# Layer 1's attention with normalised weights that carry the shared part, on column groups of TensorE

## The chip, the cores and the metric

The kernel runs on one core of a Trainium2 chip. Its engines are TensorE (PE; its weight loads are listed apart as PEld), VectorE (DVE), ScalarE (ACT), GpSimd (POOL) and SyncE (SP), which here issues most DMAs. [...] The metric is the device time of one execution in microseconds. Before the change it is 4359.8 us, the median of 3 runs (4357.15 to 4369.78).

## The reference

Two graph layers on 64 graphs of 256 nodes and 512 features, all in fp32, 8 heads of 64 features each.

```python
# layer 0: x = layernorm(x + relu(attention)), W of 512 x 64 per head
feats = einsum('bnf,hfu->bhnu', X, W)
dense = leaky_relu(e_self[..., :, None] + e_neigh[..., None, :], 0.2)
att   = softmax(dense + NEG_BIG * (1 - A), axis=-1)
out   = relu(einsum('bhij,bhju->bhiu', att, feats) + b)

# layer 1: x = layernorm(x + out @ W_out + b_out)
dots = einsum('bhid,bhjd->bhij', q, k) * scale      # q, k, v from x @ W_qkv
attn = softmax(where(m2, dots, -big), axis=-1) * 0.33
attn = attn + 0.33 * adj + 0.33 * exp(-dist)        # adj = dist = A, masked by m2
out  = einsum('bhij,bhjd->bhid', attn, v)
```

In layer 1 the last two terms of `attn` are the same for all heads of a graph: the shared part, `CT` in the kernel.

## The kernel before

A graph's 256 nodes are two tiles of 128 (T = 2), its 512 features four (C = 4). Per graph there are four lists of steps. `proj0` turns x (pt_x, L154), makes the logits (pe, L246), turns the adjacency (pa, L215) and makes from it `AT` and `CT`, makes the rows of the logits (pr, L259) and sends them through DRAM to all partitions (gs, then gb; L273 and L274), computes from them the columns ccol and wcol (nd, L279; L284, L285), and makes the features (pf, L290), which POOL scales by wcol into `V0` (L298). `attend0` makes the weights pT on DVE (L324) and multiplies them with V0 in `weighted` (av_h0, L167): a tile of weights is the stationary operand, 128 by 128, and the values of a head, 64 columns and one for the sum, the moving one. `proj1` turns the result (pt_h, L154) and makes q and k (pq, L372) and v (pv, L386). `attend1` makes the scores transposed (pz, L415), two heads on two halves of the array's rows, the exponentials on ACT (L425), and the values by the same `weighted` (av_h1, L167), with a column of ones in V1 for the sums. DVE then divides by the sums (L436 to L439). `rest` multiplies CT with V1 for all heads (pcv, L450) and DVE adds it (L457). The result o is turned (pt_o, L154, copied by ACT at L157), projected (po, L472), added and normalised.

`together` (L502) interleaves two lists by their counts of steps. In turn b, `attend0(b)` goes with `proj1(b-1)`, then `attend1(b-1)` with `proj0(b+1)`. A tile framework then sets the final order on each engine and the semaphores. On SP stand, in that order, the loads of x, adjacency and mask, gs and gb, and the store of y.

Of the kernel before, what the change touches and what calls it, by code (L numbers as in the profile page):

```python
# [8 lines left out]
FT = mybir.dt.float32  # L9
U8 = mybir.dt.uint8  # L10
AF = mybir.ActivationFunctionType
ALU = mybir.AluOpType
# [4 lines left out]
def kernel(  # L17
# [21 lines left out]

    nc = tc.nc  # L40
# [25 lines left out]
    def ps_tile(shape, tag, name):  # L66
        return psum.tile(shape, FT, tag=tag, name=name)
# [44 lines left out]
    nc.vector.memset(neg, -NEG)  # L112
    mhalf = consts.tile([P, T], FT, name="mhalf")
# [4 lines left out]
    for s, a in enumerate((a_self, a_neigh)):  # L118
        a_bc = work.tile([P, H, U], FT, tag="oT", name=f"a_bc_{s}", bufs=1)
        nc.sync.dma_start(  # L120
            a_bc.rearrange("p h u -> p (h u)"),
            a.rearrange("h u -> (h u)").partition_broadcast(P),
        )
        for c in range(C):
            prod = work.tile([P, H, U], FT, tag="o", name=f"prod_{c}_{s}")
            nc.vector.tensor_mul(prod, w0_sb[:, c], a_bc)
            nc.vector.tensor_reduce(wa[:, c, s], prod, AX.X, ALU.add)
# [16 lines left out]
    mla = consts.tile([P, T, NB], FT, name="mla")  # L144
    nc.vector.tensor_scalar_mul(mla, pm, LA)
# [51 lines left out]
    V0, GB, CCOL, AT, CT = {}, {}, {}, {}, {}  # L197

    def proj0(b):
# [3 lines left out]
        GB[b] = work.tile([P, H, N + 1], FT, tag="gb", name=f"gb_{b}")  # L203
        AT[b] = work.tile([P, T, N], FT, tag="at", name=f"at_{b}")
        CT[b] = work.tile([P, T, N], FT, tag="ct", name=f"ct_{b}", bufs=3)
# [5 lines left out]
        def adjacency():  # L211
# [12 lines left out]
            mrow = small.tile([P, N], FT, tag="mrow", name=f"mrow_{b}", bufs=2)  # L224
            nc.gpsimd.tensor_copy(mrow, MROW[b])
            for j in range(T):
# [8 lines left out]

            nc.gpsimd.tensor_scalar(
                mrow, mrow, -LA / N, LA / N, op0=ALU.mult, op1=ALU.add
            )
            for j in range(T):
                nc.gpsimd.tensor_add(CT[b][:, j, :], CT[b][:, j, :], mrow)  # L240
# [46 lines left out]
        def features(t):  # L287
# [9 lines left out]
            nc.scalar.copy(feat[:, t].rearrange("p h u -> p (h u)"), pf)  # L297
            nc.gpsimd.tensor_mul(  # L298
# [7 lines left out]
            *(lambda t=t: tr(t) for t in range(T)),  # L306
            logits,
            adjacency,
            rows,
            *(lambda t=t: features(t) for t in range(T)),  # L310
# [5 lines left out]
    def attend0(b):  # L316
        o = work.tile([P, T, F], FT, tag="o", name=f"o0_{b}")
# [36 lines left out]
        for g in range(2):  # L354
            steps += [lambda h=h: weights(h) for h in range(g * HG, (g + 1) * HG)]
            steps += [lambda g=g, t=t: values(g, t) for t in range(T)]
        return steps + [end]
# [4 lines left out]
    def proj1(b):  # L362
        hT = work.tile([P, C, N], FT, tag="xT", name=f"hT_{b}")
        QK[b] = work.tile([P, HG, 2, N], FT, tag="qk", name=f"qk_{b}")
        V1[b] = work.tile([P, T, H, UA], FT, tag="v1", name=f"v1_{b}")
# [17 lines left out]
        def values(t):  # L383
            pv = ps_tile([P, F], "mm", f"pv_{b}_{t}")
            for c in range(C):
                nc.tensor.matmul(  # L386
                    pv,
                    hT[:, c, t * P : (t + 1) * P],
                    wqkv_sb[:, c, 2].rearrange("p h u -> p (h u)"),
                    start=(c == 0),  # L390
                    stop=(c == C - 1),
                )
            nc.scalar.copy(
                V1[b][:, t, :, :U], pv.rearrange("p (h u) -> p h u", u=U)
            )
            nc.gpsimd.memset(V1[b][:, t, :, U], 1.0)

        return [
            *(lambda t=t: tr(t) for t in range(T)),
            *(lambda g=g: qk(g) for g in range(HG)),  # L400
            *(lambda t=t: values(t) for t in range(T)),
        ]


    def attend1(b):
        o = work.tile([P, T, F], FT, tag="o", name=f"o1_{b}")
        probs = {}

        def scores(g):

            pz = [ps_tile([P, T, N], "sc", f"pz_{b}_{2 * g + r}") for r in range(2)]
            for j in range(T):
                for r in range(2):
                    rows = slice(r * U, (r + 1) * U)
                    nc.tensor.matmul(  # L415
                        pz[r][:, j, :],
# [5 lines left out]
            for r in range(2):  # L422
                p = work.tile([P, T, N], FT, tag="p", name=f"p_{b}_{2 * g + r}", bufs=6)
                for j in range(T):
                    nc.scalar.activation(  # L425
                        p[:, j, :],
                        pz[r][:, j, :],
                        AF.Exp,
                        bias=hide[:, j, b : b + 1],
                    )  # L430
                probs[2 * g + r] = p

        def values(g, t):
            av = weighted(g, t, probs, V1[b], b, "h1")
            rec = small.tile([P, HG], FT, tag="rec", name=f"rec1_{b}_{g}_{t}")
            nc.vector.tensor_scalar_max(rec, av[:, :, U], TINY)  # L436
            nc.vector.reciprocal(rec, rec)
            nc.vector.tensor_scalar_mul(rec, rec, mla[:, t, b : b + 1])
            nc.vector.tensor_mul(  # L439
                o[:, t, g * HG * U : (g + 1) * HG * U].rearrange(  # L440
                    "p (h u) -> p h u", u=U
                ),
                av[:, :, :U],
                rec.unsqueeze(2).to_broadcast([P, HG, U]),
            )

        def rest(t):
            pc = ps_tile([P, H, U], "mm", f"pcv_{b}_{t}")
            for j in range(T):
                nc.tensor.matmul(  # L450
                    pc,
                    CT[b][:, j, t * P : (t + 1) * P],
                    V1[b][:, j, :, :U],
                    start=(j == 0),
                    stop=(j == T - 1),
                )
            nc.vector.tensor_add(  # L457
                o[:, t, :], pc.rearrange("p h u -> p (h u)"), o[:, t, :]
            )

        oT = work.tile([P, C, N], FT, tag="oT", name=f"oT_{b}", bufs=1)
        y = io.tile([P, T, F], FT, tag="y", name=f"y_{b}", bufs=2)
        tr = transposed(o, oT, b, "o")
# [17 lines left out]
        def end():  # L481
            layernorm(y, X1[b], b, "l1")
            nc.sync.dma_start(out[b].rearrange("(t p) f -> p t f", p=P), y)

        return [
            residual,
            lambda: scores(0),
            lambda: scores(1),
            lambda: scores(2),
            lambda: values(0, 0),  # L490
            lambda: values(0, 1),
            lambda: scores(3),
            lambda: values(1, 0),
            lambda: values(1, 1),
            *(lambda t=t: rest(t) for t in range(T)),
            *(lambda t=t: tr(t) for t in range(T)),
            *(lambda t=t: project(t) for t in range(T)),
            end,
# [3 lines left out]
    def together(one, two):  # L502
        n = len(one) + len(two)
        i = j = 0
        for _ in range(n):
            if j >= len(two) or (i < len(one) and i * len(two) <= j * len(one)):
                one[i]()
                i += 1
            else:
                two[j]()  # L510
                j += 1
# [3 lines left out]
    together(proj0(0), [])  # L515
    for b in range(NB + 1):
        if b + 2 < NB:
            load(b + 2)
        together(
            attend0(b) if b < NB else [],  # L520
            proj1(b - 1) if b >= 1 else [],
        )
        together(
            attend1(b - 1) if b >= 1 else [],
# [50 lines left out]
```

## Time and profile before

| | |
|---|---|
| median of 3 runs | 4359.8 us |
| the profiled execution | 4358.81 us |
| its span, first to last instruction | 4357.0 us |
| mean granted TensorE clock | 0.949 |
| VectorE busy | 37% |
| ScalarE busy | 23% |
| GpSimd busy | 19% |
| DMA moved, mean | 163.54 MB, 38 GB/s |

The costliest groups of TensorE by line, in us of busy time and mean length of one:

| line | what | instructions | busy | mean ns |
|---|---|---|---|---|
| L372 | q and k (pq) | 4096 | 927.4 | 382 |
| L167 | values of layer 1 (av_h1) | 4096 | 625.6 | 314 |
| L167 | values of layer 0 (av_h0) | 4096 | 487.9 | 272 |
| L386, L290, L472 | pv, pf, po | 1024 each | 463.6, 462.4, 460.2 | 595, 594, 592 |
| L415 | scores (pz) | 2048 | 427.8 | 456 |
| L450 | shared part (pcv) | 512 | 270.4 | 655 |

Matmuls overlap, so the length of one is not the time that it costs. That time is the distance from its start to the next one's, which the timeline gives.

### The profile page before, as it was taken

The numbers are of one execution on the slowest core, as the hardware profiler recorded it, in microseconds if no ns is written. First come the engines' busy times: TensorE is split into PE (matmuls) and PEld (weight loads), VectorE is DVE, ScalarE is ACT, GpSimd is POOL, SyncE is SP. The second block draws the span as 40 slices with busy tenths as digits, with TensorE's granted clock in tenths as the row PEclk, the third lists the DMA queues.
The fourth block names the chain that finished last, engine by engine and source line by source line (L and its number), as shares of the span: only waits on it lengthen the run. The fifth ranks groups of instructions, "written<-read, shape, count | busy, mean of one in ns | idle before, by whom it ended". The sixth has DMA issues, their size and how long they took to land.

```text
span 4357.0 us, 52007 instructions
## 1 busy us (share of the span) xinstructions
PE 4305.3 (99%) x20994; PEld 3126.9 (72%) x20994; DVE 1606.5 (37%) x4251; ACT 1021.7 (23%) x2241; POOL 819.7 (19%) x1286
## 2 busy tenths in 40 slices
PE   6999999999999999999999999999999999999999
PEld 4777777777777777777777777777777777777776
DVE  4333334334343333333433333334333333333342
ACT  1222222222222222222222222222222222222222
POOL 2112112111121221211212112122121121211211
PEclk9999999999999999999999999999999999999999
DMA  4111101011011010110111111101011111111100
GB/s 111 40 33 39 40 32 40 30 38 40 32 40 40 32 40 30 38 40 32 40 34 39 35 35 38 40 33 40 30 38 40 33 40 40 32 35 35 35 25 15
DMA packets 89744, 163.54 MB, mean 38 GB/s; under 512 B 30624, under 2 KB 47520, under 8 KB 81312
## 3 DMA queue, kind: packets, MB, share of 16 engines
q1 hardware_dynamic: 76208, 155.49, 11.0%
q10 hardware_dynamic: 13296, 4.72, 0.5%
q8 instruction: 166, 2.72, 0.2%
q14 instruction: 74, 0.61, 0.0%
HBM read 126.11 MB, written 34.08 MB: 37 GB/s over the span
## 4 chain that ended last, share of the span: by engine, by line
PE 98%; DMA 1%; DVE 0%; issue 0%; POOL 0%; ACT 0%; SPq 0%; ACTq 0%; POOLq 0%; DVEq 0%
PE av_h L167 24%; PE pq L372 20%; PE pv L386 10%; PE po L472 10%; PE pf L290 10%; PE pz L415 9%; PE pcv L450 6%; PE pe L246 3%; PE pt_x L154 1%; PE pa L215 1%; PE pt_o L154 1%; PE pt_h L154 1%; PE pr L259 1%; DMA gb<-gs 0%; DMA wqkv_sb<-in_L_gnn_W_qkv_dram 0%
## 5 line engine op out<-in xcount | busy, mean ns | idle before, releaser
L372 PE MATMUL pq<-hT,wqkv_sb 128*128 128x256 f32 x4096 | 927.4, 382 | 0.7 <-ACT hT L157 0.7
L372 PEld LDWEIGHTS pq<-hT,wqkv_sb 128*128 128x128 f32 x4096 | 764.8, 190 | 97.5 <-ACT hT L157 1.0
L167 PEld LDWEIGHTS av_h<-v,p 128*128 128x128 f32 x4096 | 592.1, 228 | 59.7 <-issue 42.7
L167 PE MATMUL av_h<-v,p 128*128 128x65 f32 x4096 | 625.6, 314 | 1.9
L324 DVE SCALAR_TENSOR_TENSOR pT<-gb,ccol,at 128x256 f32<-128x256 f32 x1024 | 505.5, 538 | 218.7 <-PE av_h L167 200.7
L167 PEld LDWEIGHTS av_h<-v,pT 128*128 128x128 f32 x4096 | 494.9, 192 | 42.5 <-issue 31.7
L425 ACT ACTIVATE p<-pz,hide 128x256 f32<-128x256 f32 x1024 | 401.9, 474 | 485.4 <-PE pz L415 480.7
L167 PE MATMUL av_h<-v,pT 128*128 128x65 f32 x4096 | 487.9, 272 | 3.1 <-POOL v L303 3.1
L386 PE MATMUL pv<-wqkv_sb,hT 128*128 128x512 f32 x1024 | 463.6, 595 | 0.0
L290 PE MATMUL pf<-w_sb,xT 128*128 128x512 f32 x1024 | 462.4, 594 | 0.0
L472 PE MATMUL po<-wo_sb,oT 128*128 128x512 f32 x1024 | 460.2, 592 | 0.5 <-DVE x L479 0.5
L343 POOL TENSOR_TENSOR o<-o,b_bc 128x256 f32<-128x256 f32 x256 | 197.2, 771 | 1260.3 <-DVE o L338 1252.6
L415 PE MATMUL pz<-qk 64*128 64x256 f32 x2048 | 427.8, 456 | 0.2 <-ACT p L425 0.2
L381 ACT COPY qk<-pq 128x512 f32<-128x512 f32 x256 | 150.1, 586 | 958.7 <-PE pq L372 958.7
L336 DVE RECIPROCAL rec<-av_h 128x4 f32<-128x4 f32 x256 | 46.7, 182 | 848.8 <-PE av_h L167 848.7
L472 PEld LDWEIGHTS po<-wo_sb,oT 128*128 128x128 f32 x1024 | 189.5, 190 | 215.1 <-issue 215.1
L290 PEld LDWEIGHTS pf<-w_sb,xT 128*128 128x128 f32 x1024 | 190.0, 191 | 213.4 <-issue 212.9
L436 DVE TENSOR_SCALAR rec<-av_h 128x4 f32<-128x4 f32 x256 | 41.5, 162 | 781.7 <-PE av_h L167 778.0
L386 PEld LDWEIGHTS pv<-wqkv_sb,hT 128*128 128x128 f32 x1024 | 189.8, 190 | 187.4 <-issue 184.1
L415 PEld LDWEIGHTS pz<-qk 64*128 64x128 f32 x2048 | 280.1, 211 | 57.1 <-issue 12.5
L298 POOL TENSOR_TENSOR v<-feat,wcol 128x512 f32<-128x512 f32 x128 | 163.8, 1280 | 700.6 <-ACT wcol L285 575.3
L450 PE MATMUL pcv<-v,ct 128*128 128x512 f32 x512 | 270.4, 655 | 0.0
(69 smaller groups left out, 3042.8 us busy)
## 6 DMA issues: line engine op xcount, KB each, us to landing
gb<-gs SPq DMA_DIRECT2D x64, 1028.0 KB
x<-in_x_dram SPq DMA_DIRECT2D x64, 512.0 KB
out_dram<-y SPq DMA_DIRECT2D x64, 512.0 KB
adj<-in_adj_dram SPq DMA_DIRECT2D x64, 256.0 KB
wqkv_sb<-in_L_gnn_W_qkv_dram ACTq DMA_DIRECT2D x12, 256.0 KB
mask<-in_nodemask_dram SPq DMA_DIRECT2D x64, 32.0 KB
w_sb<-in_L_gnn_W_dram SPq DMA_DIRECT2D x4, 256.0 KB
wo_sb<-in_L_gnn_W_out_dram ACTq DMA_DIRECT2D x1, 1024.0 KB
```

Of the source, the lines that this page charges most:

```text
L167: nc.tensor.matmul(av[:, k, :], weights[h][:, j, t * P : (t + 1) * P], v[:, j, h, :], start=(j == 0), stop=(j == T - 1),)
L290: nc.tensor.matmul(pf, xT[:, c, t * P : (t + 1) * P], w0_sb[:, c].rearrange("p h u -> p (h u)"), start=(c == 0), stop=(c == C - 1),)
L298: nc.gpsimd.tensor_mul(V0[b][:, t, :, :U], feat[:, t], wcol[:, t, :].unsqueeze(2).to_broadcast([P, H, U]),)
L324: nc.vector.scalar_tensor_tensor(pT[h][:, j, :], GB[b][:, h, :N], CCOL[b][:, j, h : h + 1], AT[b][:, j, :], op0=ALU.max, op1=ALU.mult,)
L343: nc.gpsimd.tensor_add(o[:, t, s], o[:, t, s], b0_bc[:, s])
L372: nc.tensor.matmul(pq[:, s, :], wqkv_sb[:, c, s, 2 * g : 2 * g + 2, :].rearrange("p h u -> p (h u)"), hT[:, c, :], start=(c == 0), stop=(c ...
L381: nc.scalar.copy(QK[b][:, g], pq)
L386: nc.tensor.matmul(pv, hT[:, c, t * P : (t + 1) * P], wqkv_sb[:, c, 2].rearrange("p h u -> p (h u)"), start=(c == 0), stop=(c == C - 1),)
L415: nc.tensor.matmul(pz[r][:, j, :], QK[b][rows, g, 1, j * P : (j + 1) * P], QK[b][rows, g, 0, :], start=True, stop=True,)
L425: nc.scalar.activation(p[:, j, :], pz[r][:, j, :], AF.Exp, bias=hide[:, j, b : b + 1],)
L450: nc.tensor.matmul(pc, CT[b][:, j, t * P : (t + 1) * P], V1[b][:, j, :, :U], start=(j == 0), stop=(j == T - 1),)
L472: nc.tensor.matmul(po, oT[:, c, t * P : (t + 1) * P], wo_sb[:, c, :], start=(c == 0), stop=(c == C - 1),)
```

## The change

Layer 1's attention becomes two lists. `softmax1` makes scores and exponentials for two heads at a time in one PSUM tile. It adds the two node tiles of the exponentials on DVE (`both`), and multiplies a block of ones (each 1/0.33) with that: the sums of four heads stand in the four column quarters of the array. Then DVE takes the reciprocals, multiplies them by the mask, and they go through DRAM to all partitions (`rs`, `rb`). `attend1` multiplies the exponentials by these on POOL, adds CT on DVE, and multiplies with the roles turned: a head's values are the stationary operand, 128 by 64, on one half of the array's columns, and the weights the moving one, 256 columns. The result comes out transposed, so ACT copies it straight to oT. The column of ones, pcv and the turning of o go.

`together` takes any number of lists, with a weight on each step. In turn b, `attend1(b-2)`, `attend0(b)` and `proj1(b-1)` go together, then `softmax1(b-1)` and `proj0(b+1)`. Features and their scaling on POOL are steps of their own. Several tiles lose their second buffer.

```diff
     def ps_tile(shape, tag, name):
-        return psum.tile(shape, FT, tag=tag, name=name)
+        return psum.tile(shape, FT, tag=tag, name=name, bufs=1 if tag == "sc" else 2)
...
+    ones = consts.tile([P, P // 4], FT, name="ones")
+    nc.vector.memset(ones, 1.0 / LA)
...
-        GB[b] = work.tile([P, H, N + 1], FT, tag="gb", name=f"gb_{b}")
+        GB[b] = work.tile([P, H, N + 1], FT, tag="gb", name=f"gb_{b}", bufs=1)
...
-        CT[b] = work.tile([P, T, N], FT, tag="ct", name=f"ct_{b}", bufs=3)
+        CT[b] = work.tile([P, T, N], FT, tag="ct", name=f"ct_{b}", bufs=4)
...
-            mrow = small.tile([P, N], FT, tag="mrow", name=f"mrow_{b}", bufs=2)
+            mrow = MF[b] = small.tile([P, N], FT, tag="mf", name=f"mf_{b}", bufs=3)
             nc.gpsimd.tensor_copy(mrow, MROW[b])
...
         return [
-            *(lambda t=t: tr(t) for t in range(T)),
-            logits,
-            adjacency,
-            rows,
-            *(lambda t=t: features(t) for t in range(T)),
+            (0.5, lambda: tr(0)),
+            (0.5, lambda: tr(1)),
+            (1.8, logits),
+            (3.5, lambda: features(0)),
+            (0.5, rows),
+            (0.5, adjacency),
+            (3.5, lambda: features(1)),
+            *((0, lambda t=t: scaled(t)) for t in range(T)),
         ]
...
-        o = work.tile([P, T, F], FT, tag="o", name=f"o0_{b}")
+        o = work.tile([P, T, F], FT, tag="o", name=f"o0_{b}", bufs=1)
...
+    def softmax1(b):
+        PROBS[b] = [
+            work.tile([P, 2, T, N], FT, tag="p", name=f"p_{b}_{g}", bufs=5)
+            for g in range(HG)
         ]
+        REC[b] = work.tile([P, 4, 2, N], FT, tag="rb", name=f"rb_{b}", bufs=1)
...
+            pz = ps_tile([P, 2, T, N], "sc", f"pz_{b}_{g}")
             for j in range(T):
                 for r in range(2):
                     rows = slice(r * U, (r + 1) * U)
                     nc.tensor.matmul(
-                        pz[r][:, j, :],
+                        pz[:, r, j, :],
                         QK[b][rows, g, 1, j * P : (j + 1) * P],
                         QK[b][rows, g, 0, :],
...
+            p = PROBS[b][g]
+            for j in range(T):
+                nc.scalar.activation(
+                    p[:, :, j, :], pz[:, :, j, :], AF.Exp, bias=hide[:, j, b : b + 1]
+                )
+            both[g] = work.tile([P, 2, N], FT, tag="both", name=f"both_{b}_{g}", bufs=3)
+            nc.vector.scalar_tensor_tensor(
+                both[g], p[:, :, 0, :], TINY, p[:, :, 1, :], op0=ALU.add, op1=ALU.add
+            )
+        def sums(pd, g):
             for r in range(2):
+                k = 2 * (g % 2) + r
+                nc.tensor.matmul(
+                    pd[k * 32 : (k + 1) * 32, g // 2, :],
+                    ones,
+                    both[g][:, r, :],
+                    start=True,
+                    stop=True,
+                    tile_position=(0, 32 * k),
+                )
+        def reciprocals():
+            pd = ps_tile([P, 2, N], "av", f"pd_{b}")
+            for g in range(HG):
+                sums(pd, g)
+            rec = work.tile([P, 2, N], FT, tag="rec1", name=f"rec1_{b}", bufs=1)
+            nc.vector.reciprocal(rec, pd)
             nc.vector.tensor_mul(
+                rec, rec, MF[b].unsqueeze(1).to_broadcast([P, 2, N])
+            )
+            rs = dram.tile([4, 2, N], FT, tag="rs", name=f"rs_{b}")
+            nc.sync.dma_start(rs, rec[0:P:32])
+            nc.sync.dma_start(
+                REC[b].rearrange("p k g n -> p (k g n)"),
+                rs.rearrange("k g n -> (k g n)").partition_broadcast(P),
+            )
+        return [
+            *((0.9, lambda g=g: scores(g)) for g in range(HG)),
+            (0.9, reciprocals),
+        ]
+    def attend1(b):
...
+        def weights(g):
+            p = PROBS[b][g]
+            for r in range(2):
+                k = 2 * (g % 2) + r
+                nc.gpsimd.tensor_mul(
+                    p[:, r],
+                    p[:, r],
+                    REC[b][:, k, g // 2, :].unsqueeze(1).to_broadcast([P, T, N]),
+                )
+                nc.vector.tensor_add(p[:, r], p[:, r], CT[b])
+        def values(g):
+            if g % 2 == 0:
+                av[0] = ps_tile([P, 2, N], "av", f"av1_{b}_{g}")
+            for j in range(T):
+                for r in range(2):
+                    nc.tensor.matmul(
+                        av[0][r * U : (r + 1) * U, g % 2, :],
+                        V1[b][:, j, 2 * g + r, :],
+                        PROBS[b][g][:, r, j, :],
+                        start=(j == 0),
+                        stop=(j == T - 1),
+                    )
+            if g % 2 == 1:
+                nc.scalar.copy(oT[:, g - 1 : g + 1, :], av[0])
...
+        steps = []
+        for g in range(HG):
+            steps += [(0, lambda g=g: weights(g)), (0.9, lambda g=g: values(g))]
         return [
+            *steps,
+            (0, residual),
+            *((3.5, lambda t=t: project(t)) for t in range(T)),
+            (0, end),
         ]
-    def together(one, two):
...
+    def together(*streams):
+        at = [0] * len(streams)
+        done = [0.0] * len(streams)
+        whole = [sum(w for w, _ in s) or 1.0 for s in streams]
+        while any(a < len(s) for a, s in zip(at, streams)):
+            k = min(
+                (k for k, s in enumerate(streams) if at[k] < len(s)),
+                key=lambda k: (done[k] + streams[k][at[k]][0] / 2) / whole[k],
+            )
+            weight, step = streams[k][at[k]]
+            step()
+            done[k] += weight
+            at[k] += 1
...
+    for b in range(NB + 2):
         if b + 2 < NB:
             load(b + 2)
         together(
+            attend1(b - 2) if 0 <= b - 2 < NB else [],
             attend0(b) if b < NB else [],
-            proj1(b - 1) if b >= 1 else [],
+            proj1(b - 1) if 0 <= b - 1 < NB else [],
         )
         together(
-            attend1(b - 1) if b >= 1 else [],
+            softmax1(b - 1) if 0 <= b - 1 < NB else [],
             proj0(b + 1) if b + 1 < NB else [],
         )
```

The order that results on TensorE for one graph, as the built program has it: the last of the sums (pd) among the transposes pt_h, pt_x, three pq groups, pt_x, half of a pz, then values of two heads, layer 0's values, values of two heads, the other half of the pz, values of four heads, layer 0's values, po, pq, layer 0's, pv, po, layer 0's, pv, pe, then pz, pf, pz, pr, pa, pf with a pz within it, and the sums. On SP: gs, gb, rs, a mask load, rb, the store of y, loads of x and adjacency.

## The prediction

> **What bounds the kernel now.** I read first the page's busy shares and its chain that ended last.
>
> ```profile
> PE 4305.3 (99%) x20994; PEld 3126.9 (72%) x20994; DVE 1606.5 (37%) x4251; ACT 1021.7 (23%) x2241; POOL 819.7 (19%) x1286
> ...
> PE 98%; DMA 1%; DVE 0%; issue 0%; POOL 0%; ACT 0%; SPq 0%; ACTq 0%; POOLq 0%; DVEq 0%
> ```
>
> TensorE is the path; every other engine is idle over 60% of the time. So the sum is made over TensorE's steps of one graph. Next, busy time by windows, one window per graph, from the first scores matmul (pz) of a graph to that of the next:
>
> ```profile
> 2060.93:2124.86 63.93, 63.90 (x329) 46.23 (x328) 24.92 (x66) 15.94 (x36) 12.76 (x21) 1.00 0.12 38
> 1990.50:2060.93 70.43, 70.40 (x329) 51.36 (x328) 24.55 (x66) 15.93 (x36) 12.83 (x21) 0.90 0.10 35
> 2124.86:2191.99 67.13, 67.10 (x330) 48.93 (x329) 24.91 (x66) 15.94 (x36) 12.66 (x21) 0.95 0.11 37
> ```
>
> The same work takes 63.93, 70.43 or 67.13 us, at a granted clock (first of the last three columns) of 1.00, 0.90 and 0.95. So 63.9 us is work and the rest a clock that is halved for a while. Over the run the first pz is at 109.45 us and that of the 63rd graph at 4277.05: 67.2 us per graph, 3.3 of them lost to the clock. Third, TensorE's timeline, for the price of each form (start, length, instructions; starts are what counts):
>
> ```profile
> 2005.03 6.92 PE L167 MATMUL av_h<-v,p 128*128 128x65 f32 x32
> ...
> 2024.84 3.60 PE L290 MATMUL pf<-w_sb,xT 128*128 128x512 f32 x8
> 2028.27 3.60 PE L472 MATMUL po<-wo_sb,oT 128*128 128x512 f32 x8
> 2031.70 1.04 PE L154 MATMUL pt_h<-ident,x 128*128 128x128 f32 x8
> ...
> 2053.40 3.68 PE L167 MATMUL av_h<-v,pT 128*128 128x65 f32 x32
> 2056.92 3.65 PE L386 MATMUL pv<-wqkv_sb,hT 128*128 128x512 f32 x8
> 2060.40 0.60 PE L154 MATMUL pt_x<-ident,x 128*128 128x128 f32 x4
> 2060.93 1.14 PE L415 MATMUL pz<-qk 64*128 64x256 f32 x8
> 2062.00 0.66 PE L154 MATMUL pt_x<-ident,x 128*128 128x128 f32 x4
> 2062.69 0.44 PE L167 MATMUL av_h<-v,p 128*128 128x65 f32 x2
> 2063.05 1.86 PE L415 MATMUL pz<-qk 64*128 64x256 f32 x8
> 2064.84 0.44 PE L167 MATMUL av_h<-v,p 128*128 128x65 f32 x2
> ```
>
> An fp32 matmul of the code is two passes here. A 512-column pass takes 0.429 us (3.43 for 8), so a 256-column one 0.216 (16 pq in 3.51); a 65-column one 0.110 (3.52 for 32)[...]; a transpose 0.11. At half clock (2005.03) the 65-column pass takes 0.21. The eight pz passes take 1.07 us in one place and 1.79 in another. In the program's order the first group alternates between row halves of the array, and eight passes are four pairs of 0.216 and some 0.2 for the excursion; the second runs one half out and then the other, unpaired.
>
> Fourth, the groups by line and the timeline of all engines, for what the new part resembles:
>
> ```profile
> L298 POOL TENSOR_TENSOR v<-feat,wcol 128x512 f32<-128x512 f32 x128 | 163.8, 1280 | 700.6 <-ACT wcol L285 575.3 <-ACT feat L297 125.3
> L336 DVE RECIPROCAL rec<-av_h 128x4 f32<-128x4 f32 x256 | 46.7, 182 | 848.8 <-PE av_h L167 848.7
> ```
>
> ```profile
> 2017.56 0.30 SPq L273 DMA_DIRECT2D gs<-grow  x1
> ...
> 2018.89 0.34 SPq L274 DMA_DIRECT2D gb<-gs  x1
> ...
> 2024.46 0.18 DVE L279 TENSOR_TENSOR nd<-ecol,gb 128x16 f32<-128x16 f32 x1 [6.33 <-DMA gb<-gs]
> 2024.68 0.22 ACT L284 ACTIVATE ccol<-nd 128x16 f32<-128x16 f32 x1 [2.39 <-DVE nd L279]
> ...
> 2025.08 1.24 POOL L298 TENSOR_TENSOR v<-feat,wcol 128x512 f32<-128x512 f32 x1 [9.68 <-ACT wcol L285]
> ```
>
> A row written to DRAM and read back to all partitions takes 1.33 us out and 5.57 from issue to use.
>
> [...]
>
> **The change, part by part, per graph at full clock.**
> Removed: 64 65-column passes of layer 1's values, 64 x 0.110 = 7.04; the shared part's pcv, 8 x 0.429 = 3.43; the transposes of o, 8 x 0.11 = 0.88. The scores' four groups, 1.07 + 1.79 + 1.75 + 1.07 = 5.68, all alternate in the new order: 4.28, so 1.40 less. Sum 12.75.
> Added on TensorE: values, 16 matmuls or 32 passes of 256 columns on column halves. If halves pair, 16 x 0.216 = 3.46; if not, 6.91; I take the pair. Sums, 16 passes, four abreast: 4 x 0.216 = 0.86; 3.46 if not. Six more excursions into another tiling (one pz split in two, three stretches of values, two of sums) at 0.2: 1.2, nothing to 2.5. In the new order the pq follow pt_h with nothing but pt_x between; hT's copy (0.59 twice, after 0.3) then shows: 0.65, where layer 0's values covered it.
> Work: 63.93 - 12.75 + 3.46 + 0.86 + 1.2 + 0.65 = 57.35 us.
>
> Other engines get shorter work than a period: POOL eight 128x512 multiplications more (10.2 us on 12.8), DVE about 4 more on 25. Their load is hidden; their latency is not. Single buffers: the next scores group waits for the exponentials of the last, some 1.3 us for a pair of heads, covered by a pf step or by pr, pa and one pf matmul (1.7); without that cover 1 us each. gb's only buffer is free when the last head's pT is made, mid-period; the one o buffer after the norm. Nothing for these. Values now wait for a chain that begins with the last sums matmul of the same graph. I follow the program's order from that instruction's start:
> - its end 0.5; [...] On DVE nd stands between reciprocal and mask multiplication; its gb (grow some 2 us after pr, then 1.33 and 5.57) lands near 4.0, so a faster reciprocal gains at most 0.9.
> - On SP the broadcast of reciprocals (rb) stands behind the load of a later mask. That load waits for the mask's cast on POOL, which stands behind both scalings of v0, which wait for wcol, hence for nd. So: nd to POOL 0.62, two scalings and copies 3.15, cast 0.40, issue 0.4: rb goes out at 9.4. Without that queue it would at 7.2 (mask product 0.7, way out 1.33).
> - rb in use 5.57 later, 14.9; eight multiplications 10.24; last addition 0.8: 26.0; last matmuls 0.6: 26.6.
> TensorE's cover from the same instant: pt_h and hT to 1.85, three pq groups 10.4, pt_x 0.4, half a pz with its switch 0.65, to 13.3; then values 3.46, layer 0's 1.76, the other pz half and switches to 19.8. So 26.6 - 19.8 = 6.8 us of waiting per graph, 4 of them in one piece. Bounds: 5.9 with the fast reciprocal[...].
> Period without clock loss: 64.15.
>
> The clock: [...] At half clock the passes from 15 to 27 us double; POOL's pace hides part of that (values take 1.73 of the 2.56 us that POOL needs for two heads). [...] I take 3.5, estimated from these: 67.65 us. No clock trace of the new order exists, so 0 to 8 is the bound.
>
> Whole run: prologue to the first pq as now, 79 us; one light period 46 and one without proj0, minus 11; 61 + 1 periods; then the last graph alone, its chain uncovered, some 87 (40 to the last sums, 27 chain, 20 projection, norm, store). 62 x 67.65 + 79 + 46 - 11 + 87 = 4395, and 1.8 outside the span (4358.8 executed against 4357.0): 4397. The profiled execution is 1 us under the median of the runs, 4359.8, so nothing is to be adjusted.
>
> **Rivals.** (a) The clock is kept, or restored at once[...]: 62 x 64.15 + 203 = 4180, faster. For it: in the trace two paired pz groups stand in stretches at full clock. [...] Also for it: the half clock of 2137.6 to 2141 (0.52 by windows) ended behind a paired pz group. It decides once the clock costs less than 2.9 us a graph. (b) Column halves don't run side by side: sums 2.6 more, last values 0.65 more, 70.9 us: 4600. For it: unpaired pz in the trace, and no column tile there. [...] (c) Wait and gain cancel: a period of 67.0 us, 4360.
>
> **How the numbers follow.** Forecast with its own side 0.47 (own range 4375 to 4510), (b) 0.15, (a) 0.31, (c) 0.07. About 0.3% is what a measurement can tell from no change. Faster 0.31, same 0.07, slower 0.62. The range goes from (a) with a fast reciprocal, 62 x 63.25 + 203 = 4125, to a little over (b).
>
> **What would show it.** Right: values' weight loads waiting for DVE's additions, 6 to 7 us a graph; POOL's multiplications waiting some 5 us on rb; the rb issue right after a mask issue; pz in 1.07; values of two heads starting within 10 ns; clock near 0.9. Wrong: TensorE idle under 3 us a graph, a mean clock of 0.97 or more, or rb issued within 8 us of the last sums.

## The result and the profile after

The changed kernel takes 4429.9 us (median of 4 runs, 4428.5 to 4433.4), the kernel before 4360.6 beside it: a ratio of 1.0157, 95% interval 1.0139 to 1.0174. It is 1.6% slower. Its profiled execution spans 4427.2 us at a mean granted clock of 0.910.

The page first: busy time of each engine, and the shares of the chain that ended last.

```profile
PE 4015.2 (91%) x18946; PEld 2591.0 (59%) x18946; DVE 2576.9 (58%) x3995; ACT 951.2 (21%) x1729; POOL 1665.8 (38%) x1670
...
DVE 0%; PE 0%; DMA 0%; issue 0%; POOL 0%; ACT 0%; POOLq 0%; DVEq 0%; SPq 0%
```

TensorE lost 2048 matmul passes and 290 us of busy time, and fell from 99% to 91% of the span. The chain reaches back only over the end of this kernel (all its shares round to 0%), so it says nothing here, and the timeline takes its place. Busy time by windows, one graph each, from one sums matmul to the next graph's (window, its length, PE, PEld, DVE, ACT, POOL, then clock, DMA share, GB/s):

```profile
2040.68:2108.81 68.13, 63.02 (x298) 40.68 (x296) 40.00 (x62) 14.84 (x27) 26.03 (x26) 0.90 0.16 52
2108.81:2176.90 68.09, 62.91 (x298) 40.54 (x294) 40.00 (x62) 14.84 (x27) 26.01 (x26) 0.90 0.15 50
```

A graph takes 68.1 us, 5.1 of them with TensorE idle, at a clock of 0.90. All but the last graphs hold 10.2 or 13.7 us of half clock (counted from the clock records), where before it was none to 13.7. The place is seen in TensorE's timeline (start, length, instructions, the wait ahead in brackets); S, the last sums of this graph, is put at 2108.81 (their two pairs of passes start at 2108.66 and 2108.90).

```profile
2110.76 10.62 PE L382 MATMUL pq<-hT,wqkv_sb 128*128 128x256 f32 x48
2121.22 0.60 PE L158 MATMUL pt_x<-ident,x 128*128 128x128 f32 x4
2121.75 0.70 PE L426 MATMUL pz<-qk 64*128 64x256 f32 x4
2126.78 1.11 PE L501 MATMUL av<-p,v 128*64 128x256 f32 x2 [4.32 <-DVE p L493]
2128.45 1.97 PE L501 MATMUL av<-p,v 128*64 128x256 f32 x6 [0.56 <-DVE p L493]
2130.35 3.68 PE L171 MATMUL av_h<-v,pT 128*128 128x65 f32 x16
2133.96 1.98 PE L501 MATMUL av<-p,v 128*64 128x256 f32 x8
2135.86 1.23 PE L426 MATMUL pz<-qk 64*128 64x256 f32 x4
2137.02 2.58 PE L501 MATMUL av<-p,v 128*64 128x256 f32 x16
2139.53 2.00 PE L171 MATMUL av_h<-v,pT 128*128 128x65 f32 x16
```

A hole of 4.3 us before the first values, and behind it everything slow: 16 passes of layer 0's values in 3.6 us where they need 1.76 at full clock. The clock records of this graph show half clock from 2124.68, within the hole, to 2138.34. What the values waited for is in the timeline of the other engines. The first eight lines are the same graph; the last five are the fourth graph from the end, where no mask (and no x or adjacency) is loaded any more (S there is 4213.88).

```profile
2109.33 3.36 DVE L462 RECIPROCAL rec<-pd 128x512 f32<-128x512 f32 x1 [0.73 <-PE pd L448]
2113.14 1.17 POOL L305 TENSOR_TENSOR v<-feat,wcol 128x512 f32<-128x512 f32 x1 [1.03 <-ACT wcol L290]
2113.44 0.51 SPq L467 DMA_DIRECT2D rs<-rec  x1
2116.17 0.65 POOL L229 CAST mf<-mask 128x256 f32<-128x256 uint8 x1
2116.85 0.33 SPq L82 DMA_DIRECT2D mask<-in_nodemask_dram  x1
2117.28 0.38 SPq L468 DMA_DIRECT2D rb<-rs  x1
2123.70 12.52 POOL L488 TENSOR_TENSOR p<-p,rb 128x512 f32<-128x512 f32 x8 [6.33 <-DMA rb<-rs]
2124.99 10.10 DVE L493 TENSOR_TENSOR p<-p,ct 128x512 f32<-128x512 f32 x6 [4.98 <-POOL p L488]
...
4220.24 0.32 SPq L468 DMA_DIRECT2D rb<-rs  x1
4224.77 7.71 POOL L488 TENSOR_TENSOR p<-p,rb 128x512 f32<-128x512 f32 x5 [2.32 <-DMA rb<-rs]
4228.05 0.65 PE L501 MATMUL av<-p,v 128*64 128x256 f32 x2 [0.52 <-DVE p L493]
4229.73 0.62 PEld L501 LDWEIGHTS av<-p,v 128*64 128x64 f32 x6 [1.48 <-DVE p L493]
4229.73 1.08 PE L501 MATMUL av<-p,v 128*64 128x256 f32 x6 [1.03 <-DVE p L493]
```

The broadcast of the reciprocals (rb) is issued right behind the load of a mask, at S+8.5, and GpSimd's multiplications begin at S+14.9. With no mask to load, rb goes out at S+6.4 and they begin at S+10.9: the wait of the first values is 0.5 us instead of 4.3, and the last three periods with all the work in them took 64.5, 63.9 and 63.7 us, with no half clock, against 68.2 in the mean of the others. The kernel so holds an experiment of its own on that queue, though three loads are gone there and not the mask's alone.

The groups by line (busy time, mean ns of one, then the idle time ahead and what ended it):

```profile
L493 DVE TENSOR_TENSOR p<-p,ct 128x512 f32<-128x512 f32 x512 | 795.6, 1602 | 314.1 <-POOL p L488 314.1
L488 POOL TENSOR_TENSOR p<-p,rb 128x512 f32<-128x512 f32 x512 | 801.7, 1601 | 422.6 <-DMA rb<-rs 422.6
L462 DVE RECIPROCAL rec<-pd 128x512 f32<-128x512 f32 x64 | 214.9, 3358 | 46.8 <-PE pd L448 46.8
```

A multiplication of 128x512 on GpSimd took 1.60 us where GpSimd's scaling of the same size took 1.28 in the kernel before, and the additions that follow on VectorE took 1.60 too, where VectorE's mask product of that size (L463) took 0.69.

### The profile page after: what moved, and what is told of

The parts are those of the page before. It is cut to its first block, busy times and chain, and to the rows that moved or that the text cites. A ratio compares the mean times of both kernels' runs of the same rounds, so it can differ in the third digit from the quotient of the medians.

```text
span 4427.2 us, 47399 instructions
## 1 busy us (share of the span) xinstructions
PE 4015.2 (91%) x18946; PEld 2591.0 (59%) x18946; DVE 2576.9 (58%) x3995; ACT 951.2 (21%) x1729; POOL 1665.8 (38%) x1670
## 5 line engine op out<-in xcount | busy, mean ns | idle before, releaser
L493 DVE TENSOR_TENSOR p<-p,ct 128x512 f32<-128x512 f32 x512 | 795.6, 1602 | 314.1 <-POOL p L488 314.1
L488 POOL TENSOR_TENSOR p<-p,rb 128x512 f32<-128x512 f32 x512 | 801.7, 1601 | 422.6 <-DMA rb<-rs 422.6
L501 PE MATMUL av<-p,v 128*64 128x256 f32 x2048 | 469.9, 534 | 334.4 <-DVE p L493 334.2
L171 PEld LDWEIGHTS av_h<-v,pT 128*128 128x128 f32 x4096 | 582.3, 223 | 105.6 <-issue 67.6
L171 PE MATMUL av_h<-v,pT 128*128 128x65 f32 x4096 | 596.1, 307 | 0.6 <-POOL v L310 0.6
L501 PEld LDWEIGHTS av<-p,v 128*64 128x64 f32 x2048 | 193.9, 186 | 553.9 <-DVE p L493 418.4
L435 ACT ACTIVATE p<-pz,hide 128x512 f32<-128x512 f32 x512 | 324.2, 684 | 219.9 <-PE pz L426 208.3
L525 DVE TENSOR_TENSOR x<-po,x 128x512 f32<-128x512 f32 x128 | 88.5, 692 | 450.8 <-PE po L518 450.8
L426 PE MATMUL pz<-qk 64*128 64x256 f32 x2048 | 338.6, 440 | 2.2 <-ACT p L435 2.2
L245 POOL TENSOR_TENSOR ct<-ct,even 128x256 f32<-128x256 f32 x128 | 101.2, 809 | 553.4 <-DVE ct L231 550.5
```

The costliest lines, as they stand in the source:

```text
L171: nc.tensor.matmul(av[:, k, :], weights[h][:, j, t * P : (t + 1) * P], v[:, j, h, :], start=(j == 0), stop=(j == T - 1),)
L426: nc.tensor.matmul(pz[:, r, j, :], QK[b][rows, g, 1, j * P : (j + 1) * P], QK[b][rows, g, 0, :], start=True, stop=True,)
L435: nc.scalar.activation(p[:, :, j, :], pz[:, :, j, :], AF.Exp, bias=hide[:, j, b : b + 1])
L488: nc.gpsimd.tensor_mul(p[:, r], p[:, r], REC[b][:, k, g // 2, :].unsqueeze(1).to_broadcast([P, T, N]),)
L493: nc.vector.tensor_add(p[:, r], p[:, r], CT[b])
L501: nc.tensor.matmul(av[0][r * U : (r + 1) * U, g % 2, :], V1[b][:, j, 2 * g + r, :], PROBS[b][g][:, r, j, :], start=(j == 0), stop=(j == T ...
```

## The experiments

Each ratio is to the kernel before, timed beside it. "Period" is the distance from one sums matmul to that of the next graph, and the half clock of a graph is summed from the clock records that lie in its period; both were counted from the traces.

**The link of rb on SyncE's queue (e1_rbq).**

```diff
-            nc.sync.dma_start(
+            nc.scalar.dma_start(
                 REC[b].rearrange("p k g n -> p (k g n)"),
```

> The changed kernel; only the read-back of the reciprocals to all partitions (rb) is issued on ScalarE's queue instead of SyncE's, so that it no longer stands behind the load of a later mask. Theory (the hole is the length of the chain from the last sums to the first values, and the queue is a link of it): rb goes out at about S+6.2 instead of S+8.5 (S = start of the last sums matmul), GpSimd's multiplications start 2.2 us earlier, the wait of the first values falls from 4.4 to about 2.1 us, the half-clock stretch may shrink with it: 2.2 to 4 us of each period of 68.1, so 4180 to 4295 us, ratio to the kernel before 0.96 to 0.985. Rival (the pace of GpSimd's multiplications and the clock set the end, whatever the start): the period stays within 0.5 us of 68.1, 4400 to 4460 us.

Measured: 4206.6 us, ratio 0.9646 (0.9627 to 0.9665). One word takes 5% off. TensorE's waits, in the view of waits (us in total, times, longest):

```profile
PE av L501 <- DVE p L493: 212.1, 266, 13.7
```

The sum was 334.2 in the changed kernel. In the mean of the graphs rb goes out 2.0 us earlier (S+6.5), and the multiplications begin 4.0 us earlier (S+11.2 instead of S+15.1): with the mask load no longer ahead of it, rb is also in use sooner after its issue (4.7 us instead of 6.6). The last addition ends at S+25.3 instead of S+29.1. Of the 59 graphs away from both ends, 43 had no half clock and a mean period of 63.79 us; 15 had 10.2 us of it and 64.91 (one had 6.8). So graphs with ten microseconds of half clock took 1.1 us more in this order. This compares graphs of one run, not two kernels; that most of the doubled passes lie beneath the pace of GpSimd is an estimate: in the changed kernel eight passes of values took 1.90 us from start to start at half clock (2133.96 to 2135.86), and GpSimd's two multiplications for them 3.20.

**Column halves one after the other (e2_unpaired).**

```diff
-            for j in range(T):
-                for r in range(2):
+            for r in range(2):
+                for j in range(T):
```

> The changed kernel; only the order of the values' matmuls within a group is changed, so that one column half runs out before the other begins (two heads one after the other instead of alternating). Theory (halves run side by side only when their passes alternate): the last groups of values, 32 passes in pairs at 0.15 to 0.17 us a pair at full clock, need twice that once they are unpaired; the groups before the last are paced by GpSimd and DVE, which hides it, so only the last two groups show: 1 to 2.5 us a period more at half clock, 4490 to 4590 us. [...] Rival (passes on column halves run one after the other in any order): no change, 4415 to 4445 us, and the start-to-start distance of two values passes as before.

Measured: 4429.6 us, ratio 1.0158 (1.0141 to 1.0175): no change, but not for the rival's reason. In TensorE's timeline of one graph:

```profile
2127.39 3.64 PE L501 MATMUL av<-p,v 128*64 128x256 f32 x8 [4.63 <-DVE p L493]
2133.56 1.09 PE L501 MATMUL av<-p,v 128*64 128x256 f32 x8
2137.43 2.01 PE L501 MATMUL av<-p,v 128*64 128x256 f32 x8 [0.60 <-DVE p L493]
```

The second line is eight passes at full clock in 1.03 us from start to start, where eight of 0.216 us one after the other would be 1.73 (an estimate from the passes of before): here they still overlap, at some 0.26 us a pair and not the 0.15 to 0.17 of the expectation, though the built program has four of one half and then four of the other. Where the second head's weights were late (first and third line) the eight took 3.57 and 1.94 us; the time of the whole is that of the changed kernel all the same, and the half clock was shorter, 618 us instead of 802 in all.

**The values laid later (e3_late_25).** In `attend1`, all steps on the weights come first, then an empty step of weight 25, and an empty step of 1.5 ahead of each group of values:

```diff
-        steps = []
+        steps = [(0, lambda g=g: weights(g)) for g in range(HG)]
+        steps += [(25, lambda: None)]
         for g in range(HG):
-            steps += [(0, lambda g=g: weights(g)), (0.9, lambda g=g: values(g))]
+            steps += [(1.5, lambda: None), (0.9, lambda g=g: values(g))]
```

> The changed kernel; only the steps of layer 1's last part are laid differently among the steps of the other graphs: GpSimd's and DVE's work on the weights first, the values' matmuls later, two groups behind layer 0's pe and softmax steps and two further on, each with other work between. No arithmetic differs. Theory (the time of the changed kernel is its waits of 6 to 7 us a graph and the half clock that they bring): the waits of values fall from 6.8 us to at most 3 us a graph, none of them in one piece of over 2 us; the clock stays at or near full (mean 0.97 or more); period 58 to 62 us, so 3800 to 4050 us, ratio 0.87 to 0.93. Rival[...]: waits fall but the half clock stays at 13 us a graph or so, period 62 to 65 us, 4050 to 4240 us.

Measured: 4009.0 us, ratio 0.9195 (0.9181 to 0.9208); mean period 61.06, clock 0.994. The chain is as long as it was (the last addition ends at S+29.6); TensorE has other work. What is left, in the view of waits:

```profile
PE av L501 <- DVE o L348: 96.7, 62, 1.6
PE av_h L171 <- POOL v L310: 58.1, 127, 0.7
```

**No addition beside the multiplications (e4_noadd).** The line `nc.vector.tensor_add(p[:, r], p[:, r], CT[b])` is left out, and with it that term of the output.

> The changed kernel without VectorE's addition of the shared part to the weights of layer 1: that term is left out of the output. Disputed cost: each of GpSimd's multiplications by rb took 1.60 us where GpSimd's other tensor-tensor operations of that size took 1.28. Theory (the two engines slow each other while they both run on tiles of this size): without the addition the multiplications take 1.25 to 1.35 us, eight of them 10.0 to 10.8 us instead of 12.5, the last values come 2.5 to 3 us earlier (the addition of 0.7 goes too) and the period falls by 2 to 4 us: 4180 to 4310 us. Rival (the operand repeated over the middle axis makes the multiplication slow by itself): they stay at 1.55 to 1.65 us and the period falls only by the last addition, 0.7 to 1 us: 4360 to 4390 us.

Measured: 4307.2 us, ratio 0.9877 (0.9862 to 0.9891). The group of multiplications:

```profile
L488 POOL TENSOR_TENSOR p<-p,rb 128x512 f32<-128x512 f32 x512 | 629.7, 1267 | 427.3 <-DMA rb<-rs 427.3
```

1.27 us again, and the time lies in the theory's range: the broadcast operand isn't what costs, the additions on VectorE beside it are.

**Both operations on VectorE (e8_dve).** `nc.gpsimd.tensor_mul` becomes `nc.vector.tensor_mul` in the same place.

> The changed kernel; only the multiplications of the weights by rb are made by VectorE instead of GpSimd, so that VectorE does both operations of a head one after the other, with nothing large beside it. Theory (GpSimd and VectorE hold each other up when both work on such tiles: 1.60 us each instead of 1.28 and 0.69): a head takes 0.69 + 0.69 = 1.4 us instead of 1.6, eight heads 11.0 us, the last values come 2.5 to 3 us earlier and the period falls from 68.1 to about 65.5 us, 4230 to 4310 us. Rival (VectorE's operations cost 1.6 us by themselves, or the order on TensorE takes back what the shorter chain gives): 4380 to 4520 us.

Measured: 4421.0 us, ratio 1.0139 (1.0122 to 1.0156). The groups:

```profile
L488 DVE TENSOR_TENSOR p<-p,rb 128x512 f32<-128x512 f32 x512 | 365.6, 744 | 231.1 <-DMA rb<-rs 231.1
L493 DVE TENSOR_TENSOR p<-p,ct 128x512 f32<-128x512 f32 x512 | 333.5, 681 | 0.0
```

0.74 and 0.68 us, as the theory says, and in the last graphs (no mask load, no half clock) the period is 61.27 where it is 63.7 in the changed kernel. But the rival holds for the time, and VectorE's timeline of one graph (S at 2111.15) shows why:

```profile
2129.97 1.28 DVE L493 TENSOR_TENSOR p<-p,ct 128x512 f32<-128x512 f32 x2
2134.92 0.18 DVE L346 RECIPROCAL rec<-av_h 128x4 f32<-128x4 f32 x1 [3.66 <-PE av_h L171]
2135.02 0.66 DVE L488 TENSOR_TENSOR p<-p,rb 128x512 f32<-128x512 f32 x1
...
2141.68 0.68 DVE L493 TENSOR_TENSOR p<-p,ct 128x512 f32<-128x512 f32 x1
```

Between the fourth and the fifth head VectorE waits 3.66 us for TensorE's values of layer 0, whose reciprocal comes first in its order. So the last addition ends at S+31.1 in the mean, 2 us later than in the changed kernel, although a head takes less. A hole of 3.1 us stays, the half clock stays (10.2 us in most graphs), halves of scores and projections stand between the values, and the graphs with mask loads take 68.5 us in the mean. The gain of 9 us lies within the two intervals.

**A filler in the hole (e5_fill3).** Three `nc.tensor.matmul(av[0], ident, REC[b][:, 0:2], ...)` ahead of the first values.

> The changed kernel with three useless 512-column matmuls (six passes, 2.6 us at full clock) in the hole ahead of the first values; they need only rb, and the values write over what they leave. Disputed cost: the half clock that follows the hole, 3.5 us a graph in the prediction's sum. In the new order half a pz and one pt_x (1.1 to 1.4 us with their change of tiling) move from the cover to behind the values, which must be paid. Theory now, after the readings of the other experiments (the pace of GpSimd's and VectorE's work on the weights, 1.6 us a head, sets the end, and the half clock is hidden beneath it but for the last group, about 1.1 us): the clock is halved for less than half as long (now 802 us in all) and the time stays nearly where it is, 4390 to 4450 us. Rival (the prediction's: the half clock costs 3.5 us on top of the wait): 4430 less 62 x (3.5 - 1.4) = 4300, 4260 to 4330 us. Third possibility: the clock is halved as before, and the time rises by up to 1.4 us a graph, to 4520 us.

Measured: 4671.6 us, ratio 1.0709 (1.0691 to 1.0727), worse than all three cases. Two lines of its timeline say where the time went:

```profile
2096.03 4.54 PE L500 MATMUL av<-rb,ident 128*128 128x512 f32 x6 [2.76 <-DMA rb<-rs]
2110.43 3.39 PE L509 MATMUL av<-p,v 128*64 128x256 f32 x16 [4.60 <-DVE o L348]
```

The hole only moved ahead of the filler, which needs rb and itself ran slowly (its six passes took 4.46 us from start to start, where six of 0.429 are 2.57), and a second hole of 4.6 us came up: the order had changed, and the buffer of the second half of the values waited for VectorE's copy of layer 0, behind the additions. It says nothing on the clock alone; the price of the half clock rests on the comparison in e1_rbq.

**The paired scores alone, in the kernel before (e6_before_pairs).**

```diff
-            pz = [ps_tile([P, T, N], "sc", f"pz_{b}_{2 * g + r}") for r in range(2)]
+            pz = ps_tile([P, 2, T, N], "sc", f"pz_{b}_{g}")
...
-                p = work.tile([P, T, N], FT, tag="p", name=f"p_{b}_{2 * g + r}", bufs=6)
+            p = work.tile([P, 2, T, N], FT, tag="p", name=f"p_{b}_{g}", bufs=3)
```

> The kernel before with one part of the change alone: the scores of a pair of heads in one PSUM tile, so that the two row halves alternate in all four groups, and the exponentials over both heads at once. Theory (alternating passes run side by side, 1.07 us for eight passes where the groups that run one half out first take 1.79): 2 x 0.7 = 1.4 us a graph less on TensorE, which is the path there: 62 x 1.4 = 87 us, 4250 to 4300 us, ratio 0.975 to 0.986. A loss could come from the single buffer of scores: the next group then waits for the exponentials, up to 1 us for each group without other work between, and the gain would fall to nothing. Rival (the split into two stretches of half a group, not the order, makes those groups slow): the time stays at 4350 to 4370 us.

Measured: 4059.4 us, ratio 0.9312 (0.9295 to 0.9328), over three times the expected gain. By windows, one graph:

```profile
2102.83:2165.18 62.35, 62.35 (x329) 44.45 (x328) 24.73 (x66) 14.65 (x28) 12.55 (x21) 1.00 0.12 39
```

62.35 against 63.93 at full clock: 1.58 us less, 1.4 of them from pairing, as expected (each of the four groups now takes 1.06 or 1.07 us from its start to the next instruction's, 4.25 in all, where it was 5.68). The rest is the clock: all 59 graphs away from the ends take 62.35 us, and the half clock fell from 450 us to 23 in all. The mean period of before was 67.2.

That pairing alone saved the clock is not shown, because the final order on TensorE changed with it. First two lines of before, in the graph that the prediction shows, then e6_before_pairs:

```profile
2068.35 1.91 PE L246 MATMUL pe<-wa,xT 128*128 128x16 f32 x16
2077.09 1.94 PE L450 MATMUL pcv<-v,ct 128*128 128x512 f32 x4
...
2109.96 1.08 PE L447 MATMUL pcv<-v,ct 128*128 128x512 f32 x2
2110.97 1.13 PE L415 MATMUL pz<-qk 64*128 64x256 f32 x8
```

In before, the first 512-column passes came 16 us after the first scores, and in between stood the scores, two of their groups unpaired, with transposes and passes of 65 and 16 columns; nearly all stretches of half clock began 9 to 11.5 us after the first scores. In e6_before_pairs 512-column passes stand between the scores, 7 us after the first. So the half clock of before goes with this stretch; whether the unpaired scores, the lack of long matmuls or something else in the order brought it is not shown.

Why the second and third group ran unpaired is in the program of before, each half with a wait of its own for ScalarE (its exponentials free the half's PSUM tile):

```
L415 Matmult pz_6_0_3024<-qk_6_2846 128x256
L415 Matmult pz_6_1_3025<-qk_6_2846 128x256
...
L415 Matmult pz_6_2_3036<-qk_6_2846 128x256 [waits Activation_49]
L415 Matmult pz_6_2_3036<-qk_6_2846 128x256
L415 Matmult pz_6_3_3037<-qk_6_2846 128x256 [waits Activation_49]
```

The trace agrees: in the graph of the prediction's lines ScalarE's exponentials of the first group end at 2063.73, and the second half of the second group starts at 2063.78, 0.73 us behind its first half:

```profile
2062.16 1.57 ACT L425 ACTIVATE p<-pz,hide 128x256 f32<-128x256 f32 x4 [0.48 <-PE pz L415]
```

**The paired order undone in the changed kernel (e10_unpaired_scores).** The same swap of the two loops as in e2_unpaired, in `scores`.

> The changed kernel with one part undone: in each scores group one row half runs out before the other begins. Theory (pairing is worth 0.7 us a group[...], as in the kernel before, where pairing alone brought 6.9 per cent): three and a half groups of each graph stand uncovered, 62 x (3.5 x 0.7 = 2.5) = 150 us for the passes, and a second stretch of half clock behind the scores, up to 2 us a graph: 4580 to 4720 us. Rival (in the changed kernel the scores have long matmuls of layer 0 between them[...]): 4560 to 4600 us, half clock still about 800 us in all. Third: pairing is worth nothing here, 4415 to 4445 us.

Measured: 4601.9 us, ratio 1.0552 (1.0532 to 1.0572). It lies in the first range, and 2 us above the second. But the passes of whole groups, which the first counted, cost nothing:

```profile
2116.97 1.14 PE L426 MATMUL pz<-qk 64*128 64x256 f32 x8
...
2138.31 1.13 PE L426 MATMUL pz<-qk 64*128 64x256 f32 x4
...
2152.30 2.07 PE L426 MATMUL pz<-qk 64*128 64x256 f32 x4
```

Whole groups still take 1.07 us from start to start with one half out first. Only the group that the scheduler splits in two stretches lost its pairs, as each stretch now holds one half: four passes last 1.13 us instead of 0.70 at full clock, and take 2.0 from start to start instead of 1.16 at half clock. That is 1.3 us a graph. The half clock grew from 802 us to 1055 in all, though the order on TensorE is otherwise that of the changed kernel, and periods lie at 69.4 to 75.2 us by how much of it they hold. So the clock part of the first theory holds in its size, but as a longer stretch and not a second one.

**Towards a fast version.** e7_late_rbq_25 is e3_late_25 with rb on ScalarE's queue.

> The two edits that won time together: the values of layer 1 laid later, and rb issued on ScalarE's queue. In the version with later values (period 61.0 us) TensorE still waits 1.6 us a graph, because VectorE's copy of layer 0's output stands behind the eight additions. Theory (rb 2 us earlier lets the additions end before that copy is due): that wait goes, period 59.3 to 59.8 us, 3900 to 3950 us, ratio 0.895 to 0.906. Rival (the copy waits for the additions wherever they stand, or the earlier multiplications hold up layer 0's scalings): no change, 3995 to 4030 us.

Measured: 4008.2 us, ratio 0.9192 (0.9176 to 0.9209): nothing. In that order GpSimd's multiplications stand behind its additions to layer 0's output and not behind rb: they begin at S+15.9 with either queue. e9_all_25 adds the multiplications on VectorE:

> Values of layer 1 laid later, rb on ScalarE's queue, and the multiplications by rb made by VectorE. Of the 61.0 us of the later-values version TensorE waits 1.55 us for VectorE's copy of layer 0's output, which stands behind the eight additions (12.4 us beside GpSimd's multiplications, whose start is set by GpSimd's own order and not by rb: so rb's queue alone gave nothing). Theory: on VectorE alone a head takes two operations of 0.61 us from start to start, eight heads 9.7 us instead of 12.4; they start at the same place (S+14.9) and end 2.7 us earlier, ahead of the moment when TensorE wants the buffer: the wait goes, period 59.3 to 59.6 us, 3895 to 3925 us, ratio 0.894 to 0.901. Rival (another wait takes its place at once, such as the buffer behind the first values): period 60.5 to 61.1, 3980 to 4015 us.

Measured: 3862.6 us, ratio 0.8857 (0.8843 to 0.8872), period 58.91: the same edit that gave at most 9 us as e8_dve gives 146 here, more than expected. In this order the eight heads follow each other on VectorE, and the last addition ends at S+25.5; what brought the gain beyond the expected 1.5 us a graph is not shown. e11_h0_2 adds an empty step of weight 2 at the head of `attend0`:

> The fastest version so far (3862.6 us, period 58.91) with layer 0's values laid one projection group later as well. There TensorE still waits 0.91 us a graph for GpSimd's scaling of layer 0's features, because layer 0's first values come 6 us after the last sums. Theory: behind the second projection group the scaling is done, the wait goes, and the order has fewer small waits: period 57.9 to 58.2 us, 3800 to 3820 us, ratio 0.871 to 0.877. Rival (layer 0's later values now wait for VectorE's pT, which the new order puts behind the work on the weights, or the buffer of values is freed too late): period 58.9 to 61 us, 3860 to 3990 us.

Measured: 3773.9 us, ratio 0.8651 (0.8637 to 0.8666), below both ranges. One graph by windows:

```profile
2083.10:2140.60 57.50, 57.21 (x297) 37.66 (x296) 37.72 (x70) 14.94 (x27) 13.89 (x19) 1.00 0.18 61
```

TensorE is idle for 0.29 us of 57.50, at full clock. This is the fastest kernel of the study: the change with its waits taken away.

## Why the prediction was right, by its steps

| per graph | predicted | measured |
|---|---|---|
| work of TensorE | 57.35 us | 57.50 (e11_h0_2, with 0.29 idle) |
| pairing of the scores | 1.40 | 1.4 (e6_before_pairs) |
| two heads' values side by side | yes, within 10 ns | 3 to 7 ns where both heads' weights are ready |
| reciprocal, 128x512 | an estimate, not shown by the trace of before | 3.36 |
| rb issued | S+9.4 | S+8.5 |
| first multiplication | S+14.9 | S+14.9 |
| the multiplications done and the last addition | S+26.0 | S+28.9 |
| first hole | 4 | 4.3 |
| period | 67.65 | 68.1 |

The bound moved as said: off TensorE's work and onto the chain from the last sums to the last values. The signs that it named came: TensorE idle 5.1 us a graph, the rb issue right behind the mask's, a clock of 0.910, GpSimd waiting 6.3 us for rb (some 5 were named), and the values' weight loads waiting for VectorE's additions, 418.4 us in all or some 6.5 a graph:

```profile
PEld av L501 <- DVE p L493: 418.4, 154, 14.3
```

The work sum held although e11_h0_2 has another order and so other changes of tiling; it supports the sum, not each of its terms. The run's rest held too: 62 x 68.1 leaves 208 us of 4430, 203 were in the prediction.

**Two terms were mis-sized, against each other, and that the total came so close is luck.** The multiplications were put at 1.28 us, the time of GpSimd's scaling of that size in before; they took 1.60, and so did the additions, the last of which ends at 2137.70. e4_noadd (1.27 us without the additions) and e8_dve (0.74 and 0.68 us with both on VectorE) show the price from both sides. Put 28.9 for 26.0 into the prediction's own balance and the wait is 9.7 us instead of 6.8. The half clock was put at 3.5 us on top, the author's estimate: TensorE was busy for 99% of the span of before, and what a hole of 4 us would do to the clock was not shown. Of 68.1 us, 57.5 of work and 9.7 of wait leave 0.9, an estimate, and the graphs of e1_rbq give 1.1 for a stretch of 10.2 us. It lasts long (13.7 us in most graphs) but mostly where the values would wait anyway: TensorE is seen idle for only 5.1 of the 9.7 us; its slower passes, such as the 16 of layer 0's values in 3.6 us for 1.76, fill part of the rest. With the first term alone set right the prediction's sum is 57.35 + 9.7 + 3.5 = 70.55 us a graph or some 4577 us, above its own range.

**Two more errors cancelled**, by luck too, at S+14.9: rb went out 0.9 us earlier than predicted (the reciprocal, an estimate of the author's that no trace showed, took 3.36 us), and it needed 6.4 us from issue to use instead of 5.57. Without loads ahead of it, in the last graphs, it needed 4.5 (4220.24 to 4224.77), and in e1_rbq, ahead of the mask load, 4.7: here the mask load cost the chain more than its place on the queue.

**The mechanism of pairing was misread.** The prediction laid the unpaired scores of before to the program's order. In e10_unpaired_scores (eight passes in 1.07 us from start to start) and e2_unpaired (1.03) the order within a stretch made no such difference; in before and in e2_unpaired the pairs failed where one half waited for its buffer or its operand (1.75 to 1.79 us and 1.94). The forecast was not hurt, since the new code happens to give both halves one PSUM tile. The loss to the clock in before (3.3 us) was rightly read, but its cause was not looked for. e6_before_pairs places it in the stretch of scores, with the part of pairing open.

**The rivals.** (a) The clock is kept: it is not (0.910). The prediction let (a) win once the clock costs less than 2.9 us a graph. It cost some 1, and the kernel was still slower, because the multiplications were. (b) Halves one after the other: refuted by starts 3 to 7 ns apart; that column halves would run side by side was the author's assumption, as before has no column tile. (c) A period of 67.0 us: missed by 1.1.

What the change gave and took, from e6_before_pairs on: with the scores paired, before needs 62.35 us a graph; the rest of the change takes TensorE's work to 57.5 and adds some 10.6 of waits and clock: 68.1.

## What to carry to other kernels

When a step is turned so that matmuls wait for a chain over other engines, count what TensorE has to do from the chain's first link to its last, and lay the consumer that much later; laying it later, freeing the chain's queue and giving the multiplications to VectorE turned 1.6% slower into 13.5% faster, with the same matmuls. Give the two halves of the array one buffer that is freed at once, since in before a half that waited for its buffer started 0.73 us behind the other, and the eight passes took 1.79 us instead of 1.07; that edit, with the order that came of it, was worth 6.9% in the kernel before, most of it through the clock. Try a shortened chain only together with a fitting order: one and the same edit was worth at most 9 us in one order and 146 in the other.

## What the runs showed of the hardware

- GpSimd's multiplications and VectorE's additions of 128x512 in fp32 took 1.60 us each while both ran, against 1.27 (e4_noadd) and 0.68 (e8_dve) apart. Done one after the other on VectorE alone, a head took less (1.42 us by the means of e8_dve) than side by side.
- Eight passes of scores on the two row halves took 1.07 us from start to start in before's first group, whose starts lie in pairs 7 ns apart, and 1.07 in e10_unpaired_scores, with four of one half ahead of four of the other in the built program. Where the second half started 0.73 us late (before, second group) they took 1.79.
- In the kernel before TensorE was busy for 99% of the span, and yet the clock was halved for 450 us. It was halved for 23 in e6_before_pairs, with paired scores and long matmuls between them; what brought the difference is not shown.
